# Two VectorE products over two PSUM banks, written as one instruction whose second pass overwrites the bank it reads

## The chip, the cores and the metric

The kernel runs on one core of one Trainium2 chip. The metric is device time in microseconds (us) of one execution, the median of three runs. Short times are given in nanoseconds (ns). The engines are called as in the profile: PE (TensorE matmul; PEld is its weight load), DVE (VectorE), ACT (ScalarE), POOL (GpSimd), SP (SyncE, which issues the DMAs).

## The reference: what is computed

Four layers are applied to an input of 4 images, 64 x 64 positions, 128 channels. Three of them (0, 1 and 3) are selective state-space blocks, and layer 2 is a gated block without a scan. The part that matters here is the scan. Each image is read in K = 4 directions (rows, columns, and both backwards), with DI = 256 channels and N = 16 states for each channel, over L = 4096 positions:

```
def step(h, t):
    x_t, d_t, B_t, C_t = t
    h = jnp.exp(d_t[..., None] * A) * h + (d_t * x_t)[..., None] * B_t[:, :, None, :]
    return (h, jnp.einsum('bkdn,bkn->bkd', h, C_t))
```

For one state n this is a first-order recurrence along the positions: the decay `exp(d*A[n])` times the old state, plus `(d*x)*B[n]`. The output sums `h[n]*C[n]` over the 16 states. Around it stand layer norms, projections, a depthwise 3 x 3 convolution, SiLU, GELU and residuals. All of it is in 32-bit floats.

## The kernel before

**Tiling.** Channels lie on the 128 partitions, in two halves m. Positions are cut into NCH = 8 chunks of CH = 512. There are 12 turns (4 images, 3 scan layers), 4 directions in each, 8 chunks in each direction: 384 chunks. A chunk is worked through in 8 **periods**, one for each half m and each group q of 4 states, so there are 3072 periods. One period scans 4 states of one half over 512 positions. A scan is one DVE instruction (`scan`, L924, `tensor_tensor_scan`), which takes the decays `da`, the input `db`, and the state that the chunk before left.

**The four states of a period** come from two places. Side 0, two states: PE makes d\*x\*B with diagonal matrices into the two-bank PSUM tile `dbp` (`pair_db`, L899), and DVE scans its two halves (L1031 and L1033 call `scan`). Side 1, two states: ACT copies d\*x of the period from the SBUF tile `du` into one PSUM bank (`lift`, L916), and DVE multiplies it by two rows of B that a DMA has spread over all partitions (`bb`): L1048 and L1049, the two lines of this change. There are two PSUM banks for it, `dv[0]` and `dv[1]`. In period i the lifted d\*x stands in bank i % 2, called `du` in the loop, and the other bank is called `db`. L1048 writes d\*x\*B of the third state into `db`. L1049 writes d\*x\*B of the fourth state over `du` itself. Then DVE scans `db` (L1050) and `du` (L1052).

**After the scans.** POOL multiplies the four state rows by C (`times_c`, L936, two instructions of 128 x 1024 for each period) and adds pairs in three or four of the eight periods (L938). PE sums the products over the states into `yp` by matmuls with the identity (`add_up`, L951). ACT saves the last state of each scan (`save`, L932).

**What ACT does in a period, in its order:** two decays of the next period (`decay`, L908, 2 x 512 exponentials), save of the period before, two more decays, save of side 0, the lift of the *next* period (L1055 calls `lift`), four diagonals for a later `pair_db` (`diagonals`, L891). The lift of the next period writes the bank that is `db` in the present one, so it may start once the scan of `db` (L1050) has read it.

**The order.** The instruction order of each engine is written out by hand in this loop, under a manual schedule. The framework puts in the semaphore waits from the tiles and regions that instructions touch; `dv` is two tiles, `dv0` and `dv1`. Between the scan's steps, at the places `other(0)` to `other(3)` and `piece(...)`, steps of the surrounding layers (norms, projections, convolution; L190 to L770) and the next chunk's preparation are put in, on all engines; their cost planner only counts matmuls. An instruction waits either with a wait of its own or, where it has more waits than it can carry, with a separate EVENT_SEMAPHORE instruction in front of it on its engine's queue.

**DVE's order in a period** is thus: scan 1 and scan 2 (from `dbp`), [L1048], [L1049], scan 3 (from the `db` bank), scan 4 (from the `du` bank), with a step of the other layers or of `leave` (L962, L964) here and there.

**Waits as the built program has them.** L1048 waits for three things: the lift, the rows of B (every second period), and an older scan of the bank that it writes. L1049 waits for nothing. Scan 3 waits for L1048, and for POOL or ACT beside; the wait for L1048 is a separate EVENT_SEMAPHORE in 2985 periods, and carried by the scan in 87. Scan 4 waits for L1049. The lift waits for scan 3 of the period before its own.

Of the kernel before, what the change touches and what calls it, by code (L numbers as in the profile page):

```python
# [13 lines left out]
F32 = mybir.dt.float32  # L14
# [11 lines left out]
CH = 512  # L26
NCH = L // CH
RPC = CH // W
P = 128
# [48 lines left out]
def cost(step):  # L78

    return getattr(step, "matmuls", 0) or (0.05 if step is empty else 0.25)  # L80
# [6 lines left out]
def alike(a, b):  # L87
    return empty in (a, b) or hasattr(a, "matmuls") == hasattr(b, "matmuls")


def when(place):

    chunk, place = divmod(place - 1, 4 * len(ROOM))
    i, number = divmod(place, 4)
    return chunk + (sum(ROOM[:i]) + ROOM[i] * number / 4) / sum(ROOM)
# [3 lines left out]
def vss_stack_kernel(ctx: ExitStack, tc: tile.TileContext, x: bass.AP, weights, out: bass.AP, n_batch=B, layers=(0, 1, 2, 3)):  # L99
# [6 lines left out]
    nc = tc.nc  # L106
# [660 lines left out]
    for turn, (e, i) in enumerate(turns):  # L767

        for nth, k in enumerate((1, 3, 0, 2) if turn else (0, 1, 3, 2)):
            for ci in range(NCH):  # L770
                s = SimpleNamespace(turn=turn, e=e, v=wt[i], layer=i, nth=nth, k=k, ci=ci)
# [17 lines left out]
    def meanwhile(turn):  # L789

        chunk, end = 4 * 8, 4 * 8 * (per_turn - 2) - 4
        if not turn:

            first = [(row, n * chunk, (n + 1) * chunk - 2) for n, row in enumerate(opening[4:])]
            rest = combine(1, psums), combine(3, psums), *between(turns[1][0], None, 0, psums)
            return first + spaced(rest, first[-1][2], end)
        rows = after(*turns[turn - 1])
        if turn + 1 == len(turns):

            last = [(row, n * chunk + 8, (n + 1) * chunk + 8) for n, row in enumerate(after(*turns[turn]), 3 * NCH + 1)]  # L800
            return spaced(rows, 8, last[0][1]) + last
        if turns[turn + 1][1] == 0:
            rows += between(turns[turn + 1][0], None, 0, psums)
        return spaced(rows, 8, end)
# [4 lines left out]
    def scans(pool, ring, deep, psum):  # L809
# [60 lines left out]
        def spread(s, q, b):  # L870

            rows_of, at, count = ((s.bb, CQ * q + 2, CQ - 2), (s.cb, CQ * q, CQ))[b]
            rows_of[q] = pool.tile([P, count, CH], F32, tag="bc"[b] + "b", name="bc"[b] + "b")
            row = R + b * N + at
            nc.sync.dma_start(
                out=rows_of[q], in_=s.xd_d[s.k // 2 : s.k // 2 + 1, row : row + count].to_broadcast([P, count, CH])
            )

        def place(s, i):


            q = i // 2
            return q, (i + q + s.flip) % 2
# [11 lines left out]
        def pair_db(s, i):  # L895
            q, m = place(s, i)
            s.db = psum.tile([P, CH, 2], F32, tag="dbp", name="dbp")
            for t in range(4):
                nc.tensor.matmul(  # L899
                    s.db[:, t * P : (t + 1) * P, :], s.duT[:, t, m, :], s.diag[q][:, t], start=True, stop=True  # L900
                )

        def decay(s, i, side):
            q, m = place(s, i)
            da = ring.tile([P, 2, CH], F32, tag="da", name="da")
            for j in range(2):
                n = CQ * q + 2 * side + j
                nc.scalar.activation(da[:, j], s.delta[:, m], AF.Exp, scale=s.v["a"][:, s.k, m, n : n + 1])  # L908
            return da

        dv = [psum.tile([P, CH], F32, name=f"dv{j}") for j in range(2)]

        def lift(s, i):
            nc.scalar.copy(dv[i % 2], s.du[:, place(s, i)[1]])  # L916

        def scan(s, i, side, j, da, db):
            q, m = place(s, i)
            if j == 0:  # L920
                s.h[i, side] = deep.tile([P, 2, CH], F32, tag="h", name="h")
            n = CQ * q + 2 * side + j
            init = 0.0 if s.first else s.state[:, m, n : n + 1]
            nc.vector.tensor_tensor_scan(  # L924
                s.h[i, side][:, j, s.step], da[:, j, s.step], db[:, s.step], init, ALU.mult, ALU.add
            )

        def save(s, i, side):
            if not s.last:
                q, m = place(s, i)  # L930
                n = CQ * q + 2 * side
                nc.scalar.copy(s.state[:, m, n : n + 2].unsqueeze(2), s.h[i, side][:, :, s.end : s.end + 1])  # L932

        def times_c(s, i, side):
            hc = s.hc[i, side] = deep.tile([P, 2, CH], F32, tag="hc", name="hc")
            nc.gpsimd.tensor_mul(hc, s.h[i, side], s.cb[i // 2][:, 2 * side : 2 * side + 2, :])  # L936
            if side == 1 and i in PAIRED:
                nc.gpsimd.tensor_add(hc, hc, s.hc[i, 0])  # L938
# [32 lines left out]
        s = chunks[0]  # L971
# [13 lines left out]
        for at, (s, i) in enumerate(periods):  # L985
            then = periods[at + 1] if at + 1 < len(periods) else None
            if i == 0:
                nxt = chunks[at // 8 + 1] if at // 8 + 1 < len(chunks) else None
                if nxt:
                    pro, nxt.dt = prologue(nxt), s.dt  # L990
                s.state = pool.tile([P, 2, N], F32, tag="state", name="state") if s.first else before[0].state
                if at % (8 * per_turn) == 0:
                    segments = [
                        SimpleNamespace(todo=steps, done=0, dense=True, total=len(steps), frm=frm, to=to)

                        if to - frm <= 4 * 8
                        else SimpleNamespace(
                            todo=steps, done=0, dense=False, total=sum(map(cost, steps)), frm=when(frm), to=when(to)
                        )
                        for steps, frm, to in meanwhile(s.turn)  # L1000
                    ]

            def piece(number):

                if nxt and number in PIECES:
                    next(pro)

            def other(number):

                place = at % (8 * per_turn) * 4 + number  # L1010
                for g in segments:
                    gone = place if g.dense else when(place)
                    while g.todo and g.done < g.total * (gone - g.frm) / (g.to - g.frm):
                        step = g.todo.pop(0)
                        g.done += 1 if g.dense else cost(step)
                        step()

                        if gone < g.to and not g.dense and (step is empty or g.todo and not alike(step, g.todo[0])):
                            break

            da_next = [None, None]
            spreads = (s, i // 2 + 1) if i < 7 else (nxt, 0)
            if i % 2 == 0 or not spreads[0]:
                spreads = None
            if then:
                da_next[0] = decay(*then, 0)
            if before:
                save(*before, 1)
            if spreads:
                spread(*spreads, 0)  # L1030
            scan(s, i, 0, 0, da[0], s.db[:, :, 0])  # L1031
            other(0)
            scan(s, i, 0, 1, da[0], s.db[:, :, 1])  # L1033
            times_c(s, i, 0)

            if before and i % 2 == 0:
                add_up(*before, 0)
            if then:
                pair_db(*then)
            piece(2 * i)  # L1040
            other(1)
            if spreads:
                spread(*spreads, 1)
            if then:
                da_next[1] = decay(*then, 1)
            save(s, i, 0)
            du, db = dv[i % 2], dv[1 - i % 2]
            nc.vector.tensor_mul(db, du, s.bb[i // 2][:, 0])  # L1048
            nc.vector.tensor_mul(du, du, s.bb[i // 2][:, 1])  # L1049
            scan(s, i, 1, 0, da[1], db)  # L1050
            other(2)
            scan(s, i, 1, 1, da[1], du)  # L1052
            times_c(s, i, 1)
            if then:
                lift(*then)  # L1055

            q, half = (i + 2 + i % 2) // 2, 1 - i % 2
            if q < 4:
                diagonals(s, q, half)
            elif nxt:  # L1060
                diagonals(nxt, q - 4, half)
            if i < 2 and full:
                leave(*full.pop(0))
            if before:
                add_up(*before, *((2, 3) if i % 2 else (1, 2, 3)))
            piece(2 * i + 1)
            other(3)
            da = da_next
            before = (s, i)
            if then and then[0].turn != s.turn:  # L1070
                assert not any(g.todo for g in segments)
# [100 lines left out]
```

## Time and profile before

| | |
|---|---|
| three timed runs | 22,064.29, 22,066.67, 22,081.29 us; median 22,066.67 us |
| profiled execution, first to last instruction (span) | 22,070.4 us |
| mean granted TensorE clock | 0.963 |
| instructions in the profile | 216,982 |
| busy: ACT, POOL | 18,587.9 us (84%), 19,266.5 us (87%) |
| DMA | 3,060 MB, mean 139 GB/s |
| mean start of one period to that of the next | 7.10 us |

The profile gives one execution. Its span is the only time of that execution, and it lies 3.7 us above the median of the three timed runs and inside them; nothing has to be added to it. A group row reads: line, engine, operation, output<-inputs, shapes, count | busy us, mean ns of one | idle time of the engine just before, and what ended most of it. A wait row reads: who waited <- for whom: us in total, times, longest. A timeline row reads: start us, length us, engine, line, operation, names, shapes, how many instructions were merged into the row, and in brackets the idle time before it with its releaser (only idle times over 0.15 us are shown).

### The profile page before, as it was taken

To read this page: it belongs to the slowest core of one execution; us is meant where nothing else is said; L and a number is where in the kernel's file an instruction comes from. 1 tells how busy PE (TensorE), PEld (TensorE's weight loads), DVE (VectorE), ACT (ScalarE), POOL (GpSimd) and SP (SyncE) were. 2 spreads that over 40 slices of the span, in tenths; PEclk is the share of its full clock that TensorE was granted. 3 is DMA by queue.
4 is the path that set the end of the run, shared out by engine and by line. 5 is a ranking of instruction groups with operands and counts; after the bars stand their busy time and mean duration, and the time that the engine had idled before them with its cause. 6 is when DMAs were issued, how large, how long until landed. Compare 5 with 4: busy or idle time off the path is not lost. (4 is left out here: it accounts for less than half of the span.)

```text
span 22070.4 us, 216982 instructions
## 1 busy us (share of the span) xinstructions
PE 19694.9 (89%) x58234; PEld 10511.8 (48%) x58234; DVE 19479.8 (88%) x20186; ACT 18587.9 (84%) x40022; POOL 19266.5 (87%) x8862
## 2 busy tenths in 40 slices
PE   7898998898889889889989988989988988898897
PEld 3444444444444444444444444444444444444443
DVE  5999999999888888899889899989988888889996
ACT  6888888888888888888888888888888888888887
POOL 5999899899888888888889888988988888889996
PEclk9999999999999999999999999999999999999999
DMA  4444444444335434434534544444443453354342
GB/s 109 147 149 146 135 144 149 136 139 151 130 131 139 142 128 140 146 133 145 144 138 144 145 141 140 141 147 134 142 149 127 137 143 137 131 140 145 140 144 101
DMA packets 2437559, 3060.10 MB, mean 139 GB/s; under 512 B 1753840, under 2 KB 1790064, under 8 KB 2238192
## 3 DMA queue, kind: packets, MB, share of 16 engines
q1 hardware_dynamic: 2436336, 3046.22, 44.4%
q8 instruction: 472, 7.73, 0.1%
q14 instruction: 751, 6.15, 0.1%
HBM read 2784.41 MB, written 261.49 MB: 138 GB/s over the span
## 5 line engine op out<-in xcount | busy, mean ns | idle before, releaser
L936 POOL TENSOR_TENSOR hc<-h,cb 128x1024 f32<-128x1024 f32 x6144 | 14399.4, 2363 | 2276.5 <-DVE h L924 1113.1
L951 PE MATMUL yp<-hc,ident 128*128 128x512 f32 x18432 | 9062.1, 618 | 688.3 <-POOL hc L938 546.8
L908 ACT ACTIVATE da<-delta,w 128x512 f32<-128x512 f32 x12288 | 8148.0, 713 | 543.5 <-DVE h L924 530.5
L924 DVE TENSOR_TENSOR_SCAN h<-da,state,dbp 128x512 f32<-128x512 f32 x5376 | 6573.3, 1262 | 818.9 <-PE dbp L899 576.0
L899 PE MATMUL dbp<-diag,duT 128*128 128x256 f32 x24576 | 6012.6, 388 | 652.4 <-DVE h L924 560.1
L924 DVE TENSOR_TENSOR_SCAN h<-da,state,dv 128x512 f32<-128x512 f32 x5376 | 6589.4, 1264 | 0.0
L899 PEld LDWEIGHTS dbp<-diag,duT 128*128 128x128 f32 x24576 | 4675.2, 193 | 2921.3 <-issue 1673.1
L951 PEld LDWEIGHTS yp<-hc,ident 128*128 128x128 f32 x18432 | 3483.6, 196 | 4999.1 <-issue 3656.8
L891 ACT ACTIVATE diag<-ident,bt 128x128 f32<-128x128 f32 x12288 | 3952.1, 402 | 0.0
L938 POOL TENSOR_TENSOR hc<-hc 128x1024 f32<-128x1024 f32 x1536 | 3624.1, 2359 | 120.4
L1048 DVE TENSOR_TENSOR dv<-dv,bb 128x512 f32<-128x512 f32 x3072 | 2088.3, 680 | 945.9 <-ACT dv L916 730.3
L916 ACT COPY dv<-du 128x512 f32<-128x512 f32 x3072 | 1799.1, 586 | 984.6 <-DVE h L924 977.1
L1049 DVE TENSOR_TENSOR dv<-dv,bb 128x512 f32<-128x512 f32 x3072 | 2118.4, 690 | 0.0
L444 PE MATMUL gap<-halo,cw 128*128 128x512 f32 x3456 | 1750.8, 604 | 5.9 <-DVE cen L281 2.2
L924 DVE TENSOR_TENSOR_SCAN h<-da,dbp 128x512 f32<-128x512 f32 x768 | 891.1, 1202 | 250.7 <-PE dbp L899 166.9
L859 POOL TENSOR_TENSOR du<-delta,xs 128x512 f32<-128x512 f32 x768 | 979.9, 1276 | 31.8 <-ACT delta L847 31.8
L842 PE MATMUL ps_dt<-xd,dt_w 8*128 8x512 f32 x1536 | 881.2, 654 | 130.2 <-ACT delta L845 78.2
L932 ACT COPY state<-h 128x2 f32<-128x2 f32 x5376 | 964.3, 179 | 0.0
L444 PEld LDWEIGHTS gap<-halo,cw 128*128 128x128 f32 x3456 | 628.1, 191 | 654.8 <-issue 617.8
L924 DVE TENSOR_TENSOR_SCAN h<-da,dv 128x512 f32<-128x512 f32 x768 | 893.8, 1204 | 0.0
L845 ACT ACTIVATE delta<-ps_dt,w 128x512 f32<-128x512 f32 x768 | 524.9, 683 | 103.0 <-PE ps_dt L842 98.2
L865 PEld LDWEIGHTS ps_duT<-ident,du 128*128 128x128 f32 x3072 | 383.7, 142 | 321.9 <-issue 255.8
(122 smaller groups left out, 11686.6 us busy)
## 6 DMA issues: line engine op xcount, KB each, us to landing
cb<-xd_d SPq DMA_DIRECT2D x1536, 1024.0 KB
bb<-xd_d SPq DMA_DIRECT2D x1536, 512.0 KB
xs<-x_row_d SPq DMA_DIRECT2D x192, 512.0 KB
xs<-x_col_d SPq DMA_DIRECT2D x192, 512.0 KB
x_col_d<-down SPq DMA_DIRECT2D x192, 256.0 KB
x_row_d<-wide SPq DMA_DIRECT2D x96, 512.0 KB
y_d<-y_sb SPq DMA_DIRECT2D x96, 512.0 KB
y<-y_d SPq DMA_DIRECT2D x96, 512.0 KB
```

The costliest lines, as they stand in the source:

```text
L444: nc.tensor.matmul(z.ps, z.cw[:, m, t, :], z.halo[c][:, dy : dy + RPC, dx : dx + W], start=(t == 0), stop=(t == 8),)
L859: nc.gpsimd.tensor_mul(s.du[:, m], s.delta[:, m], s.xs[:, m])
L891: nc.scalar.activation(s.diag[q][:, t, :, j], ident, AF.Copy, scale=s.bt[:, t, CQ * q + j : CQ * q + j + 1])
L899: nc.tensor.matmul(s.db[:, t * P : (t + 1) * P, :], s.duT[:, t, m, :], s.diag[q][:, t], start=True, stop=True)
L908: nc.scalar.activation(da[:, j], s.delta[:, m], AF.Exp, scale=s.v["a"][:, s.k, m, n : n + 1])
L916: nc.scalar.copy(dv[i % 2], s.du[:, place(s, i)[1]])
L924: nc.vector.tensor_tensor_scan(s.h[i, side][:, j, s.step], da[:, j, s.step], db[:, s.step], init, ALU.mult, ALU.add)
L936: nc.gpsimd.tensor_mul(hc, s.h[i, side], s.cb[i // 2][:, 2 * side : 2 * side + 2, :])
L938: nc.gpsimd.tensor_add(hc, hc, s.hc[i, 0])
L951: nc.tensor.matmul(getattr(s, f"yp{m}"), ident, s.hc[i, side][:, j], start=opens, stop=closes)
L1048: nc.vector.tensor_mul(db, du, s.bb[i // 2][:, 0])
L1049: nc.vector.tensor_mul(du, du, s.bb[i // 2][:, 1])
```

## The change

The two one-bank tiles become one tile of two banks, and L1048 and L1049 become one instruction. Its output goes over both banks, first `db`, then `du` (in even periods the bank order is reversed by a step of -1). Its first input is `du`, read twice with a step of 0. Its second input is the two rows of B. In the second pass each element of `du` is read and overwritten in place. `lift` and the scans address halves of the one tile. In the changed kernel L1048 sets `both` and L1049 is the one product; all other line numbers stay.

```
-        dv = [psum.tile([P, CH], F32, name=f"dv{j}") for j in range(2)]
+        dv = psum.tile([P, 2, CH], F32, name="dv")

         def lift(s, i):
-            nc.scalar.copy(dv[i % 2], s.du[:, place(s, i)[1]])
+            nc.scalar.copy(dv[:, i % 2], s.du[:, place(s, i)[1]])
...
-            du, db = dv[i % 2], dv[1 - i % 2]
-            nc.vector.tensor_mul(db, du, s.bb[i // 2][:, 0])
-            nc.vector.tensor_mul(du, du, s.bb[i // 2][:, 1])
+            du, db = dv[:, i % 2], dv[:, 1 - i % 2]
+            both = dv if i % 2 else dv[:, ::-1]
+            nc.vector.tensor_mul(both, du.unsqueeze(1).to_broadcast([P, 2, CH]), s.bb[i // 2])
             scan(s, i, 1, 0, da[1], db)
             other(2)
             scan(s, i, 1, 1, da[1], du)
```

The built programs of both kernels hold the same instructions in the same order on PE, ACT, POOL and SP, apart from waits. On DVE one instruction goes in each period: 3072 products of 128 x 1024 in place of 6144 of 128 x 512. The waits differ as follows in the program after. The product no longer waits for an older scan. Scan 3 waits for the product, which is now the instruction just in front of it, again with a separate EVENT_SEMAPHORE in 2985 periods and its own wait in 87. Scan 4 has no wait of its own left in all but one period. The lift's wait is for scan 4 of the period before its own, in place of scan 3, in all periods: scan 3 raises a semaphore of its own in only 218 of 3072 periods, and the first decay after the lift, which in the program before waited for scan 4, has no wait for DVE left.

## The prediction

> **What bounds the kernel now.** I read the busy times first, then DVE's waits, then DVE's and ACT's timelines around the two products. From the page:
>
> ```profile
> PE 19694.9 (89%) x58234; PEld 10511.8 (48%) x58234; DVE 19479.8 (88%) x20186; ACT 18587.9 (84%) x40022; POOL 19266.5 (87%) x8862
> ...
> L924 DVE TENSOR_TENSOR_SCAN h<-da,state,dv 128x512 f32<-128x512 f32 x5376 | 6589.4, 1264 | 0.0
> ...
> L1048 DVE TENSOR_TENSOR dv<-dv,bb 128x512 f32<-128x512 f32 x3072 | 2088.3, 680 | 945.9 <-ACT dv L916 730.3
> L916 ACT COPY dv<-du 128x512 f32<-128x512 f32 x3072 | 1799.1, 586 | 984.6 <-DVE h L924 977.1
> L1049 DVE TENSOR_TENSOR dv<-dv,bb 128x512 f32<-128x512 f32 x3072 | 2118.4, 690 | 0.0
> ```
>
> Four engines lie between 84% and 89%: no single bound, but a ring in which each waits for the others now and then. In 1858 of the 3072 periods DVE has no idle time over 0.15 us; there the period costs what DVE's queue costs. DVE's longest waits, one answer:
>
> ```profile
> DVE h L924 <- PE dbp L899: 742.8, 557, 8.6
> DVE dv L1048 <- ACT dv L916: 730.3, 328, 7.5
> ```
>
> To learn how much a longer DVE queue costs the whole, I walked the trace back from one of the last scans to the start, at each step to the releaser where the instruction had waited, else to the one before it on its engine. The way passes from L1049 to scan 3 in **957 periods (0.31)**, and from scan 3 into the lift 78 times. 0.31 is the share that a small delay costs; the 1858 periods without a wait (0.60) bound the share upward, since other ways are nearly as long.
>
> **The product: two instructions against one.** DVE's timeline of an undisturbed period:
>
> ```profile
> 10340.18 0.67 DVE L1048 TENSOR_TENSOR dv<-dv,bb 128x512 f32<-128x512 f32 x1
> 10340.76 0.69 DVE L1049 TENSOR_TENSOR dv<-dv,bb 128x512 f32<-128x512 f32 x1
> 10341.36 2.44 DVE L924 TENSOR_TENSOR_SCAN h<-da,state,dv 128x512 f32<-128x512 f32 x2
> ```
>
> Lengths overlap: each starts about 90 ns before the one in front ends. Medians over all periods, start to start: L1048 to L1049 582 ns, L1049 to scan 3 597 ns, so **1179 ns** from product to scan 3. Scan 3 to scan 4 takes 1187 ns, where scan 4 carries a wait long fulfilled, and scans without one follow at 1171. For the new 128 x 1024 product the nearest rows are L379 and L396, 128 x 1024 with one PSUM input and a broadcast:
>
> ```profile
> L379 DVE TENSOR_TENSOR y<-y,gap x96: 1181/1197/1223, 1978.6 to 22014.5; 128x1024 f32<-128x1024 f32 x96
> ```
>
> Their output is in SBUF; to PSUM, 512 wide, L1048 takes 675 ns median against L265's 671, and L1049, which overwrites its own bank, 690. I take **1210 ns**, between 1181 and 675 + 690 = 1365.
>
> **The wait that is added.** Scan 3 needs the product's result. Before, it waited for L1048 with all of L1049 in between, so the wait was over by then. Now the product stands just in front. The nearest row of a DVE instruction waiting for the one right before it:
>
> ```profile
> 6376.05 0.69 DVE L640 TENSOR_REDUCE sums<-g 128x1 f32<-128x512 f32 x1 [3.41 <-POOL g L637]
> 6376.77 0.16 DVE L652 TENSOR_REDUCE mean<-sums 128x1 f32<-128x8 f32 x1
> ```
>
> L640 ends at 6376.74 and L652 starts 34 ns later, in all four layers' cases, not 90 ns earlier. There the wait is carried by the instruction. In 2985 of 3072 periods scan 3's wait for the product is a separate EVENT_SEMAPHORE, and that is dearer. Where a scan was released by PE through such an instruction (545 cases) it starts 121 to 123 ns after the semaphore rises; a DVE instruction that carries the wait itself (354 and 85 cases of ACT) starts 23 to 24 ns after. An example with ACT, DVE's row and then ACT's:
>
> ```profile
> 12810.09 2.45 DVE L924 TENSOR_TENSOR_SCAN h<-da,state,dbp 128x512 f32<-128x512 f32 x2 [1.43 <-ACT da L908]
> ```
> ```profile
> 12808.65 1.32 ACT L908 ACTIVATE da<-delta,w 128x512 f32<-128x512 f32 x2
> ```
>
> The decay ends at 12809.97, the scan starts 0.12 later. Semaphores of DVE and ACT rise about 10 ns before the recorded end, so I take scan 3 at **112 ns after the product's end** (bounds: 90 before it, 134 after). Product to scan 3 is then 1210 + 112 = 1322 against 1179, **+143 ns**; scan 4's lost wait gives 16 back. Net **+127 ns a period**, 390 us over 3072 (ends: 1181 - 90 - 1179 - 16 = -104 ns; 1365 + 134 - 1179 - 16 = +304 ns). I take a share of 0.40, between 0.31 and 0.60 and nearer the walked one: 0.40 x 390 = **+156 us** (with 0.31 and 0.60: 121 to 234). Behind the waiting scan on DVE stand scan 4 and all of the next period; POOL's L936 (1113.1 us of waits for DVE's scans already) and ACT's saves wait for them.
>
> Here the Trainium skill speaks for the change. "VectorE: DVE Perf Modes", section "The DRAIN you can't avoid", says that eight copies took the same time with a semaphore after each as with one at the end: "the semaphore costs nothing extra here". By that, the product would cost 1210 - 90 = 1120 ns to scan 3, 59 less than now. The L652 row and the separate waits disagree with it here by 124 and about 200 ns, and I go by the rows.
>
> **The lift's wait.** It moves from scan 3 to scan 4, 1.17 us later. Now:
>
> ```profile
> 10342.66 0.59 ACT L916 COPY dv<-du 128x512 f32<-128x512 f32 x1 [0.95 <-DVE h L924]
> 10343.19 1.28 ACT L891 ACTIVATE diag<-ident,bt 128x128 f32<-128x128 f32 x4
> 10344.37 1.32 ACT L908 ACTIVATE da<-delta,w 128x512 f32<-128x512 f32 x2
> ```
>
> Scan 3 ended about 10342.63; the lift came 33 ns after. Lift, four diagonals and two decays are queued behind the wait on ACT. 61% of all lifts start before scan 4's end, and would have to start later by 1.87 ms in total, 0.63 us a period. Directly that hurts little: two scans (2.36 us) stand between scan 4 and the next product, and where the lift was early, the product started over 1.8 us after its end in 99% of cases. What is lost is ACT's lead before a burst (a GELU or table load). Pushing each early lift back in ACT's own timeline, and letting ACT's idle time absorb the push, makes 220 products late by 143 us and 32 scans by 20 us in total: 163 us. The walk gives 78 x 1.17 = 91 us. Bounds: 0 to 163, and I take **+130 us**, between both. If ACT's cover were gone, each early lift would cost up to 1.17 us.
>
> **What costs nothing.** 3072 DVE instructions and their semaphores go; their time is in the 1179. The product's dropped wait for an older scan was long fulfilled: scan to product is 1171 ns, as between scans without waits. The rows of B are asked for and released at the same place, so the bb DMA (196.1 us of DVE waits) stays. No DMA, matmul or POOL instruction moves.
>
> **Sum:** +156 + 130 = +286 us on the profiled 22,070.4, which lies 3.7 us above the median of the runs; on the median, 22,066.7 + 286 = **22,353 us (+1.3%)**. With both terms at their ends, +121 + 0 to +234 + 163, this case covers 22,188 to 22,464.
>
> **Rivals.**
> - *Faster: the wait for the instruction in front is free.* Then product to scan 3 is 1210 - 90 = 1120 ns, 59 under 1179, and scan 4 gives 16: -75 ns a period. With 0.31 that is -71 us, with 0.60 -138, with every period -230. At 0.31 and a lift that ACT's idle time (16% of the span) hides: 21,996 us. It decides from the point at which product to scan 3 falls under 1195 ns. For it: all other neighbours on DVE overlap by 90 ns. Against it: those have no such wait; L652, which has one, does not overlap. **0.10.**
> - *Absorbed.* Scan 3 is late, but DVE's 2.59 ms of idle time and ACT's lead swallow nearly all: 22,066.7 to 22,111, say 22,090. For it: 1214 periods have a DVE wait already. Against it: 957 products on the walked way, with no slack. **0.06.**
> - *Every period pays.* DVE becomes the bound, the lift's delay adds to it: 390 + 163 = 553, **22,620 us**. For it: 1858 periods without a wait, and PE and POOL both wait for DVE's scans. Against it: PE (89%) is on the way for a third of the time, and does not slow down. **0.12**, for all beyond 22,464.
> - That the product is not one instruction: the built program has it as one, in all periods.
>
> **How the numbers follow.** My case has 0.72: 22,353. "Within 0.2%" means +-44 us, about what a measurement of this kernel tells from no change. Faster 0.10, same 0.06, slower 0.72 + 0.12 = 0.84. The range leaves out the faster case and the upper part of "every period pays": low 22,110 (wait cheap at +34 ns after the end, 1244 - 1179 - 16 = +49 ns, 0.31 of it 47 us, no lift cost: 22,113), high 22,640 (both ends of that case; the dearest product and wait, +304 ns, give 0.31 x 934 + 130 = +420, 22,487, and stay inside).
>
> **What would show it.** In the changed profile: L1049 at 1181 to 1230 ns; scan 3 about 110 ns after its end instead of 90 before; the lift's idle time before it grown beyond 984.6 us, released at scan 4; more products waiting for L916 than 328; DVE's busy time *lower*, its idle time higher. If scan 3 overlaps the product's end, the first step is wrong; if the lift's waits grow but the products' do not, the second; if the product is near 1365 ns, overwriting in place is dear.

## The result and the profile after

| | before | after |
|---|---|---|
| median of the runs (4 each) | 22,065.48 us | **22,457.34 us** (22,449.14 to 22,459.11) |
| ratio, 95% interval | | 1.0176 (1.0162 to 1.0191) |
| profiled span | 22,070.4 us | 22,457.3 us (+386.9) |
| product to scan 3, start to start, median | 1179 ns | 1312 ns |
| product's end to scan 3's start | -93 ns (overlap) | +104 ns |
| scan 3 to scan 4, median | 1187 ns | 1197 ns |
| lifts that start before scan 4 ends | 61% | none |
| ACT idle before the lift | 984.6 us | 2408.0 us |

The kernel is 392 us slower. From the page of the changed kernel:

```profile
PE 19795.8 (88%) x58234; PEld 10518.5 (47%) x58234; DVE 19591.0 (87%) x17114; ACT 18558.4 (83%) x40022; POOL 19280.0 (86%) x8862
...
L924 DVE TENSOR_TENSOR_SCAN h<-da,state,dv 128x512 f32<-128x512 f32 x5376 | 6612.0, 1268 | 282.7 <-DVE dv L1049 8.7
...
L1049 DVE TENSOR_TENSOR dv<-dv,bb 128x1024 f32<-128x1024 f32 x3072 | 3725.9, 1213 | 1019.8 <-ACT dv L916 815.2
...
L916 ACT COPY dv<-du 128x512 f32<-128x512 f32 x3072 | 1803.8, 587 | 2408.0 <-DVE h L924 2364.4
```

No engine took over: all four shares fell. The scan's row from `dv` had 0.0 us of idle time in front of it; now it has 282.7, and its releaser is the product. Waits under 0.15 us are not put down to a releaser, so only 8.7 us stand behind the product's name. But 104 ns, 3072 times, make 320 us, and these stand in the idle columns of this row (282.7) and of the scans of first chunks (42.1). DVE's timeline of a quiet period shows it directly:

```profile
10492.24 1.21 DVE L1049 TENSOR_TENSOR dv<-dv,bb 128x1024 f32<-128x1024 f32 x1
10493.55 2.45 DVE L924 TENSOR_TENSOR_SCAN h<-da,state,dv 128x512 f32<-128x512 f32 x2
10495.91 2.43 DVE L924 TENSOR_TENSOR_SCAN h<-da,state,dbp 128x512 f32<-128x512 f32 x2
10498.25 1.21 DVE L1049 TENSOR_TENSOR dv<-dv,bb 128x1024 f32<-128x1024 f32 x1
```

The product ends at 10493.45 and scan 3 starts at 10493.55. Every other neighbour here still starts before the one in front ends: 10493.55 + 2.45 = 10496.00, and the next scan starts at 10495.91. ACT's timeline of the same time:

```profile
10494.63 0.18 ACT L932 COPY state<-h 128x2 f32<-128x2 f32 x1
10496.03 0.59 ACT L916 COPY dv<-du 128x512 f32<-128x512 f32 x1 [1.23 <-DVE h L924]
10496.56 1.28 ACT L891 ACTIVATE diag<-ident,bt 128x128 f32<-128x128 f32 x4
```

ACT sits idle for 1.23 us until scan 4 has ended at 10496.00, and only then does the lift, with the diagonals and decays queued behind it. Part of the idle time before the lift only moved there: ACT's idle time before the decays (L908) fell from 543.5 to 127.4 us. Lift and decays together rose from 1528.1 to 2535.4 us.

**Where the 387 us are.** Each period can be cut at DVE's five starts. The mean of each stretch, before and after, times 3072:

| stretch on DVE | before, ns | after, ns | us in all |
|---|---|---|---|
| product to scan 3 | 1184.8 | 1318.6 | +411 |
| scan 3 to scan 4 | 1258.6 | 1260.6 | +6 |
| scan 4 to the next scan 1 | 1833.3 | 1785.2 | -148 |
| scan 1 to scan 2 | 1250.8 | 1250.5 | -1 |
| scan 2 to the product (here the lift is waited for) | 1576.6 | 1615.7 | +120 |

The wait in front of scan 3 is paid in full by DVE. In front of the next scan 1, 148 us come back: waits for PE fell by 52.5 us (742.8 to 690.3), those for ACT's decays by 47.5 (104.7 to 57.2), the rest is spread over others. That what a scan waits for is late by less when the scans are late too would fit, but was not tried. DVE's waits, changed kernel:

```profile
DVE dv L1049 <- ACT dv L916: 815.2, 408, 7.5
DVE h L924 <- PE dbp L899: 690.3, 523, 8.6
```

Products late for the lift rose from 328 to 408.

### The profile page after: what moved, and what is told of

Read it like the earlier page. It is cut to its first block, busy times and chain, and to the rows that moved or that the text cites. A ratio compares the mean times of both kernels' runs of the same rounds, so it can differ in the third digit from the quotient of the medians.

```text
span 22457.3 us, 212350 instructions
## 1 busy us (share of the span) xinstructions
PE 19795.8 (88%) x58234; PEld 10518.5 (47%) x58234; DVE 19591.0 (87%) x17114; ACT 18558.4 (83%) x40022; POOL 19280.0 (86%) x8862
## 5 line engine op out<-in xcount | busy, mean ns | idle before, releaser
L908 ACT ACTIVATE da<-delta,w 128x512 f32<-128x512 f32 x12288 | 8131.2, 712 | 127.4 <-DVE h L924 118.7
L924 DVE TENSOR_TENSOR_SCAN h<-da,state,dv 128x512 f32<-128x512 f32 x5376 | 6612.0, 1268 | 282.7 <-DVE dv L1049 8.7
L1049 DVE TENSOR_TENSOR dv<-dv,bb 128x1024 f32<-128x1024 f32 x3072 | 3725.9, 1213 | 1019.8 <-ACT dv L916 815.2
L916 ACT COPY dv<-du 128x512 f32<-128x512 f32 x3072 | 1803.8, 587 | 2408.0 <-DVE h L924 2364.4
L932 ACT COPY state<-h 128x2 f32<-128x2 f32 x5376 | 962.2, 179 | 0.0
L924 DVE TENSOR_TENSOR_SCAN h<-da,dv 128x512 f32<-128x512 f32 x768 | 897.3, 1208 | 42.1 <-DVE dv L1049 3.6
L865 PE MATMUL ps_duT<-ident,du 128*128 128x128 f32 x3072 | 467.7, 275 | 99.5 <-ACT duT L867 95.2
```

What stands on the lines that cost most here:

```text
L916: nc.scalar.copy(dv[:, i % 2], s.du[:, place(s, i)[1]])
L924: nc.vector.tensor_tensor_scan(s.h[i, side][:, j, s.step], da[:, j, s.step], db[:, s.step], init, ALU.mult, ALU.add)
L1049: nc.vector.tensor_mul(both, du.unsqueeze(1).to_broadcast([P, 2, CH]), s.bb[i // 2])
```

## The experiments

Theory A: two waits cost the time. Scan 3 waits for the instruction just in front of it on its own engine, and the lift waits 1.17 us longer, which takes ACT's lead (the time by which ACT's work is ready before it is needed). Rival B: it is nearly all the lift. Rival C: it is the two-bank instruction itself. All times are medians; the kernel before stood at 22,061 to 22,066 us beside each group of runs. In brackets stand the ratio to it and its 95% interval.

### The wait in front of scan 3 alone: two_tiles_scan_du_first

```
-            nc.scalar.copy(dv[i % 2], s.du[:, place(s, i)[1]])
+            nc.scalar.copy(dv[0], s.du[:, place(s, i)[1]])
...
-            nc.vector.tensor_mul(db, du, s.bb[i // 2][:, 0])
-            nc.vector.tensor_mul(du, du, s.bb[i // 2][:, 1])
-            scan(s, i, 1, 0, da[1], db)
+            nc.vector.tensor_mul(db, du, s.bb[i // 2][:, 1])
+            nc.vector.tensor_mul(du, du, s.bb[i // 2][:, 0])
+            scan(s, i, 1, 0, da[1], du)
...
-            scan(s, i, 1, 1, da[1], du)
+            scan(s, i, 1, 1, da[1], db)
```

(with `du, db = dv[0], dv[1]` in all periods)

> The kernel before, with its two tiles and two products, but the lifted bank is the same in all periods and is scanned first: scan 3 reads what the second product has just written. So only the wait for the instruction in front is added: the lift waits for scan 3 as before, nothing is merged. Theory A: product to scan 3 is 582 + 690 + 104 = 1376 ns against 1179, +197 ns a period, 605 us over all periods; with a share of 0.31 to 0.60 the time is 22,250 to 22,430 us. Rival B: about 22,066 us, since the lift is not moved. Rival C (the two-bank instruction itself is slow): 22,066 us as well.

Measured: 22,266.40 us, ratio 1.0090 (1.0074 to 1.0107), **+201 us** with nothing merged and the lift still behind scan 3. Product to scan 3 is 1375 ns. DVE's timeline:

```profile
10339.83 0.69 DVE L1049 TENSOR_TENSOR dv<-dv,bb 128x512 f32<-128x512 f32 x1
10340.62 2.45 DVE L924 TENSOR_TENSOR_SCAN h<-da,state,dv 128x512 f32<-128x512 f32 x2
```

0.69 us long, and the scan starts 0.79 after its start, where it was 0.60. The stretch is longer by 195 ns in the mean, scan 3 to scan 4 by 5 more; 200 x 3072 = 614 us, and a third of it (0.33) reaches the end. So B and C, which both expected 22,066 us, can't be the whole cause.

### The lift's wait alone: lift_after_scan4

```
-            if before:
-                save(*before, 1)
...
+            save(s, i, 1)
             if then:
                 lift(*then)
...
-        save(*before, 1)
```

> The kernel before, with one edit on ACT: the save of side 1, which waits for scan 4, is put in front of the lift and no longer into the next period. So the lift waits for scan 4, as in the changed kernel, in the 7 of 8 chunks of a direction that save; DVE's instructions and waits are those of the kernel before, product to scan 3 stays at 1179 ns. Theory A: the lift's part is 60 to 160 us: 22,125 to 22,225 us, products waiting for L916 rise from 730 us to between 800 and 900. Rival B: nearly all of the 392 us, 22,370 us or more.

Measured: 22,276.36 us, ratio 1.0095 (1.0080 to 1.0110), **+211 us**, more than A's upper end. Product to scan 3 is 1180 ns, as before. The wait is now on the save in front of the lift. ACT's waits:

```profile
ACT state L932 <- DVE h L924: 1884.7, 1435, 5.0
...
ACT dv L916 <- DVE h L924: 144.7, 169, 3.0
```

The lift starts 134 ns after scan 4's end in the median of the waiting cases, not 34 to 90 as in the changed kernel, since the save (L932) comes first; and in one chunk of eight there is no save. So this run is near the changed kernel's lift, and not the same. DVE's waits for the lift, the products' row and the scans', then the scans' row of the kernel before:

```profile
DVE dv L1046 <- ACT dv L916: 854.5, 384, 7.6
...
DVE h L924 <- ACT dv L916: 68.4, 58, 4.6
```
```profile
DVE h L924 <- ACT dv L916: 19.0, 18, 1.3
```

The products of the kernel before waited 730.3 us for it. So products and scans together wait 174 us more (922.9 against 749.3). Of DVE's other waits some fell and some rose: those for PE's `dbp` from 742.8 to 768.4 us, those for a step of a surrounding layer on ACT (`cen`, L281) from 116.2 to 147.0.

By an estimate, the two parts alone make 201 x 136/200 = 137 us (136 ns is the changed kernel's lengthening of the same two stretches) and 211, together 348 of the 392. Neither makes the 392 alone.

### The wait twice: one_tile_two_products

```
-            both = dv if i % 2 else dv[:, ::-1]
-            nc.vector.tensor_mul(both, du.unsqueeze(1).to_broadcast([P, 2, CH]), s.bb[i // 2])
+            nc.vector.tensor_mul(db, du, s.bb[i // 2][:, 0])
+            nc.vector.tensor_mul(du, du, s.bb[i // 2][:, 1])
```

> The one two-bank tile of the changed kernel, but two products of 128x512 again. In the built program the second product now waits for the first, and scan 3 for the second, each standing just in front; the lift still waits for scan 4. So the suspected wait is paid twice. Theory A (the wait for the instruction in front is the main cost): product to scan 3 is 675 + 33 + 690 + 104 = 1502 ns against 1312 in the changed kernel, +190 ns a period, 584 us over all periods; with a share of 0.38 to 0.60 the time is 22,680 to 22,810 us. Rival B (the lift's later start is the main cost, the wait in front of scan 3 is hidden): the lift is as in the changed kernel, so about 22,457 us, within 40 us.

Measured: 22,703.01 us, 1.0288 (1.0273 to 1.0303), +246 us over the changed kernel. Product to scan 3 is 1511 ns (1502 forecast). The lift is where it was, so B, which expected no change, falls. Both stretches together are 197 ns longer than there, and of 197 x 3072 = 605 us, 0.41 reaches the end.

### How the wait is carried: wait_carried_by_scan, and its control before_h_one_tile

```
-            if j == 0:
-                s.h[i, side] = deep.tile([P, 2, CH], F32, tag="h", name="h")
+            if j == 0 and side == 0:
+                both = pool.tile([P, 4, CH], F32, tag="h", name="h")
+                s.h[i, 0], s.h[i, 1] = both[:, 0:2], both[:, 2:4]
```

> The changed kernel, with the states h of both sides of a period in one tile of 4 rows (two buffers) in place of four tiles of 2 rows. POOL's release of h is then waited for at scan 1 alone, and in the built program scan 3 carries its wait for the product itself in 3071 periods, without an EVENT_SEMAPHORE in front. Theory A: scan 3 starts about 33 ns after the product's end and not 104; product to scan 3 is 1241 ns, 71 less, 218 us over all periods, so 83 to 131 us less than the changed kernel: 22,325 to 22,375 us. Rival B: about 22,457 us. A POOL that frees h later than scan 1 needs it would hide a part; it would show as more waits of scan 1 for L936.

> The control of the run whose scan 3 carries its wait: the kernel before, unchanged but for the states h of both sides of a period in one tile of 4 rows (two buffers). Theory A: this edit by itself does little. Scan 1 waits for the later of POOL's two releases, which raised DVE's waits for POOL by some 60 us in that run: 22,066 to 22,120 us. If this kernel were slower by 100 us or more, the carried wait would be worth more than the 105 us seen; if it were faster by 100, nothing.

Measured: 22,352.67 us (1.0130, 1.0115 to 1.0145), 105 us under the changed kernel; the control 22,064.15 us (1.0001, 0.9992 to 1.0010), so the edit by itself does nothing that can be seen. DVE's timeline of the first (all lines are one higher there):

```profile
10459.98 1.21 DVE L1050 TENSOR_TENSOR dv<-dv,bb 128x1024 f32<-128x1024 f32 x1
10461.22 2.45 DVE L925 TENSOR_TENSOR_SCAN h<-da,state,dv 128x512 f32<-128x512 f32 x2
```

The scan starts 0.03 after the product's end: 35 ns in the median, against 104 with the separate instruction. The changed kernel holds the same comparison in itself: product to scan 3 is 1312 ns in the 2985 periods with the separate instruction and 1244 in the 87 where the scan carries the wait. So the 104 is two things: about 35 for waiting for the instruction in front, about 70 for doing it through a separate EVENT_SEMAPHORE. The 70 ns x 3072 = 216 us are worth 105 us here, a share of 0.49.

### Giving ACT its lead back: diagonals_before_lift, on the kernel before too, and with the carried wait

```
-            if then:
-                lift(*then)

             q, half = (i + 2 + i % 2) // 2, 1 - i % 2
...
                 diagonals(nxt, q - 4, half)
+            if then:
+                lift(*then)
```

> The changed kernel with one edit on ACT: the four diagonals (1.28 us), which wait for no scan of this period, stand in front of the lift. ACT can then work while scan 4 ends, and has its lead of about 1.2 us back. DVE's instructions and waits stay: product to scan 3 1312 ns. Theory A (of the 392 us, about 211 are the lift's later start, by ACT's lead): 100 to 211 us less than the changed kernel, 22,246 to 22,357 us. If what costs is only that the lift itself comes later before the product, the time stays at 22,457 us or rises, since the lift can only become later by this.

> The same edit in the kernel before, where the lift waits for scan 3: ACT sat idle before the lift for 977 us, and could do the diagonals then; the product started 2.8 us after the lift's end in the median, so a lift later by up to 1.28 us mostly still comes in time. Theory A: 0 to 150 us less than the kernel before, 21,916 to 22,066 us. Rival: the slack of the lift counts, not ACT's lead: 22,066 to 22,250 us.

> Both repairs in the changed kernel: scan 3 carries its wait for the product (22,353 us by itself), and the diagonals stand in front of the lift. Theory A: the gains add up, another 100 to 211 us: 22,142 to 22,253 us. What is then left over the kernel before is product to scan 3, 1244 against 1179 ns, 65 ns x 3072 x 0.33 to 0.48 = 66 to 96 us, and what is left of the lift.

Measured: the changed kernel 22,343.04 us (1.0122, 1.0109 to 1.0136), 114 us less; the kernel before 22,120.48 us (1.0023, 1.0014 to 1.0032), 54 us *more* than without the edit, so A's hope there failed; both repairs 22,248.80 us (1.0082, 1.0068 to 1.0096), 209 us less, the sum of 105 and 114 but for 10. The lift comes later in both kernels, and products wait longer for it (815.2 to 1124.6 us in the changed one, 730.3 to 1113.7 in the kernel before). The same edit helps where ACT sits idle for scan 4 and hurts where the lift could go at scan 3. In the changed kernel more products waited, and yet the time fell. So a part of what the lift's wait costs there, 114 us net by this edit, comes from the work that stands behind the lift in ACT's queue, and not from a lift that is late for its product. That this holds for the whole of the lift's part is not shown: in lift_after_scan4, 174 us of the rise stood in waits for the lift. DVE's waits of the changed kernel with the edit:

```profile
DVE dv L1049 <- ACT dv L916: 1124.6, 497, 7.9
DVE h L924 <- PE dbp L899: 549.5, 428, 8.6
```

The second row shows part of what was won: 140.8 us less waiting for PE, whose matmuls need the diagonals. The waits for the diagonals on PE's side, first in the changed kernel, then with the edit:

```profile
PEld dbp L899 <- ACT diag L891: 152.7, 187, 4.6
...
PE dbp L899 <- ACT diag L891: 90.0, 61, 4.2
```
```profile
PEld dbp L899 <- ACT diag L891: 78.9, 101, 3.8
...
PE dbp L899 <- ACT diag L891: 46.2, 34, 3.4
```

Both are about halved. By the stretches used above, DVE's way from scan 4 to the next scan 1 became 256 us shorter in all, and that from scan 2 to the product 187 us longer. No version beats the kernel before.

### Covering the wait with scan 2: product_before_scan2, and its control before_products_before_scan2

The product stands between scan 1 and scan 2.

```
             other(0)
+            du, db = dv[:, i % 2], dv[:, 1 - i % 2]
+            both = dv if i % 2 else dv[:, ::-1]
+            nc.vector.tensor_mul(both, du.unsqueeze(1).to_broadcast([P, 2, CH]), s.bb[i // 2])
             scan(s, i, 0, 1, da[0], s.db[:, :, 1])
```

> The changed kernel, with the product moved up between scan 1 and scan 2, so that scan 2 covers the wait for it; the lift still waits for scan 4 and is now needed 1.17 us sooner. Theory A: product to scan 2 is about 1120 ns and no scan starts late behind it, 194 ns a period less than in the changed kernel; with a share of 0.40 this gives 240 us back. Against it stands the lift: with the slack that the changed kernel's trace shows, 651 products would be late by 621 us more in all, of which a third to two thirds reach the end, 200 to 400 us. So 22,400 to 22,650 us, with product waits for L916 over 1,300 us in place of 815. Rival B (the lift's lead matters little, as I first had it): 22,200 to 22,250 us.

> The kernel before, with its two products moved up between scan 1 and scan 2; the lift waits for scan 3 as before, and no wait for the instruction in front is added. It prices the place by itself: the lift is needed 1.18 us sooner, PE gets the bank of dbp 1.18 us later, POOL the first two states 1.18 us later. If the place is what made the changed kernel with the product moved up so slow (22,942 us, where I expected at most 22,650), this kernel is slower than the kernel before by 400 us or more. If it was the lift's wait for scan 4 together with the earlier need, this kernel stays within 200 us of the kernel before.

Measured: 22,941.63 us (1.0400, 1.0384 to 1.0415), 292 us over the top of what I expected. DVE's timeline shows that the wait was covered as meant:

```profile
10496.13 1.22 DVE L1035 TENSOR_TENSOR dv<-dv,bb 128x1024 f32<-128x1024 f32 x1
10497.25 1.28 DVE L924 TENSOR_TENSOR_SCAN h<-da,state,dbp 128x512 f32<-128x512 f32 x1
10498.43 2.43 DVE L924 TENSOR_TENSOR_SCAN h<-da,state,dv 128x512 f32<-128x512 f32 x2
```

Product to scan 2 is 1116 ns. But the control, two products at the same place in the kernel before, takes 22,888.51 us (1.0377, 1.0359 to 1.0396): the place alone costs 827 us. PE's waits in that control, the first against 560.1 us in the kernel before:

```profile
PE dbp L899 <- DVE h L924: 2062.7, 1357, 7.1
```

PE gets `dbp` back 1.2 us later, which I had left out of the sum. At this place, where scan 2 covers the wait, the change costs 53 us (22,941.6 against 22,888.5) and not 392. The two were measured in different groups of runs and their intervals overlap, so the 53 is hardly told from nothing; that it is far below 392 is clear. How much of it is the lift's wait, against the 63 ns a period saved (1116 for 1179), wasn't tried.

### No lift at all: no_lift_two_products and no_lift_product_before_scan2

```
-            nc.vector.tensor_mul(db, du, s.bb[i // 2][:, 0])
-            nc.vector.tensor_mul(du, du, s.bb[i // 2][:, 1])
+            lifted = s.du[:, place(s, i)[1]]
+            nc.vector.tensor_mul(db, lifted, s.bb[i // 2][:, 0])
+            nc.vector.tensor_mul(du, lifted, s.bb[i // 2][:, 1])
...
-            if then:
-                lift(*then)
```

(The second kernel has one product over both banks, which reads `s.du` in the same way, between scan 1 and scan 2.)

> The kernel before without the lift: the two products read d*x from its SBUF tile and write the two banks; all is computed. ACT has 1,799 us less to do and DVE waits for no lift (730 us of waits before). Theory A (the lift's place in ACT's queue is what ties DVE to ACT): faster than before by 100 to 600 us, 21,470 to 21,970 us, unless an engine's rows get longer because DVE now reads two SBUF tiles; then L1048 and L936 would show it (680 and 2363 ns before). Rival: the time stays within 50 us of 22,066, because PE (89%) or POOL (87%) take over.

> One product over both banks, d*x read from SBUF without a lift, placed between scan 1 and scan 2. So neither of the two suspected waits is left, and the merged product's gain stays: product to scan 2 about 1120 ns against 1179 for the two products, and the next scans without a late start, some 75 ns a period. Theory A: faster than the kernel without the lift that keeps two products by 70 to 140 us. If the merged instruction were slow by itself, it would be slower than that one.

Measured: 27,518.14 us (1.2479, 1.2458 to 1.2499) and 24,287.60 us (1.1009, 1.0993 to 1.1025). Both say nothing on the change, because another cost swamps it. DVE's and POOL's timelines of the first:

```profile
10021.32 0.78 DVE L1048 TENSOR_TENSOR dv<-du,bb 128x512 f32<-128x512 f32 x1
10022.01 2.85 DVE L1049 TENSOR_TENSOR dv<-du,bb 128x512 f32<-128x512 f32 x1
```
```profile
10019.19 5.12 POOL L936 TENSOR_TENSOR hc<-h,cb 128x1024 f32<-128x1024 f32 x2 [0.29 <-DVE h L924]
10024.27 2.81 POOL L487 TENSOR_TENSOR y<-y,wide 128x1024 f32<-128x1024 f32 x1
```

The second product takes 2.85 us in place of 0.69. It ends at 10024.86, 0.55 us after POOL's pair ended at 10024.31, as if it had waited for POOL's instruction to end and then run. This is the rule and not one case: 2,798 of the 3,072 second products take over 1 us, and nine in ten of these end 0.55 to 0.56 us after the end of a POOL instruction. POOL's next (L487) took 2.81 in place of 2.36. That the second kernel is 3,231 us faster than the first fits with one product a period that can meet POOL, in place of two; it doesn't tell what a merged product is worth.

## Why the prediction was right, step by step

- **What bounds the kernel** (a ring of four engines, a third to six tenths of a DVE delay reaching the end): right. The share was 0.33, 0.41 and 0.49 in three experiments; I took 0.40. With some 30 us of uncertainty on each ratio, the three shares are not told apart. The same walk back through the changed trace passes through 1170 products (0.38) against 957.
- **The product's length**: 1210 ns forecast, 1208 median. Overwriting the bank in place and the reversed bank order cost nothing seen. (The 671 ns beside it in the prediction are L265's mean; its median is 664.)
- **The added wait**: 112 ns after the product's end forecast, 104 measured; product to scan 3 1322 against 1312. This step carried the sign of DVE's term. The Trainium skill, "VectorE: DVE Perf Modes", section "The DRAIN you can't avoid", measured on eight copies that the semaphore costs nothing extra. That did not hold here: the wait costs about 125 ns where the scan carries it (35 after the end against 90 before it) and 195 with a separate instruction.
- **Scan 4's lost wait** (16 ns back): wrong. Scan 3 to scan 4 rose from 1187 to 1197 ns. In the runs whose scan 3 starts after an idle time it is 1196 to 1197, in lift_after_scan4 and before_h_one_tile 1187, in the two with the product before scan 2 1171 to 1172. Net the period's DVE queue grew by 136 ns, not 127.
- **The lift's wait**: the mechanism was right, the term was too small: +130 forecast, 211 alone. I had counted late products and scans with DVE's other waits held fixed (163 us), and then taken less. That count was near what lift_after_scan4 shows (174 us more of waits for the lift); what it left out are DVE's other waits behind ACT's queue, for PE, which needs the diagonals behind the lift, and for L281. (The 1.87 ms of later starts are 0.61 us a period, not 0.63; nothing was worked out from it.)
- **Nothing else costs**: right as far as seen; waits for the bb DMA are 192.6 against 196.1 us.
- **What would show it**: DVE's busy time should have fallen. It rose, 19,479.8 to 19,591.0 us, because two overlapping rows count once where they overlap, and product and scan 3 no longer overlap. The other signs came as written.
- **The sum**: 156 + 130 = 286 forecast, 392 measured. About 137 + 211 = 348 are shown one at a time; the 44 left over lie within the uncertainty (some 30 us on each ratio) and were not separated. The term of the wait was thus near its estimate (156 against 137), and most of the 106 us by which the sum was low are the lift's. That a queue with less lead pays a larger share of a DVE delay (0.33 with the lift at scan 3, 0.41 and 0.49 with it at scan 4) fits, but is argued only.

## What to carry to other kernels

Before two instructions are merged, look at who reads the result and how far behind it stands: the second of the two was the cover for the first one's result, and what the merge saves (63 ns a period, 1116 against 1179, where the wait is covered) was less than the wait that it uncovered (104 ns after the end in place of 93 before). Look also at what the merge does to the tiles: two buffers that become one are released together, so an engine that could start after the first reader now waits for the last, and a wait of 1.2 us on an engine that seems to have time to spare can still be paid by others, who wait for what is queued behind it (211 us here, tried alone). Count waits under the profile's listing limit by start-to-start distances, since 104 ns a period is in no list of waits.

## What the runs showed of the hardware that I had not expected

- A DVE product with two SBUF inputs and a POOL product with two SBUF inputs do not run side by side: 2.85 us against 0.69, ended 0.55 us after POOL's end. "SBUF — State Buffer" in the Trainium skill, section "Who interferes with whom", says that a DVE instruction with two SBUF inputs contends with a POOL instruction that reads SBUF, and calls the shared access an exclusive lock; the rows agree. With the lift, where one input is in PSUM, the products show none of it.
- A wait that a DVE instruction carries itself ends 23 to 24 ns before its start; one in a separate EVENT_SEMAPHORE in front of a scan that PE releases 120 to 123 ns before, in 545 cases before and 505 after. The difference shows only while the wait is still open. When it is long over, L1049 to scan 3 is 597 ns either way: with the separate instruction in the kernel before (in all but some 85 periods) and with the wait carried by the scan in before_h_one_tile (in 2995).
- A scan that follows a scan which started after an idle time starts 1196 to 1197 ns after it, not 1171 or 1187. Why, was not tried.
